# Two attention layers on one core: the last two batches' keys and values made as a pair, four heads at a time

## The chip, the cores and the metric

The kernel runs on one NeuronCore of one Trainium2 chip, in fp32 throughout. The metric is the device time of one execution in microseconds; before the change the median of three runs is 2086.57 us (2086.13 to 2086.70).

## The reference

Two cross-attention layers follow each other. Each has a query projection, keys and values for 77 text tokens and 645 image tokens of the same batch, 20 heads of 32, an output projection and a residual. The second layer adds a semantic term to the image scores and multiplies the image probabilities by a mask. What matters here is this part of each layer (the second layer's weights are not transposed; the text part is a softmax of its own, and its output is added):

```python
q = x @ Wq                     # 8 batches, 100 rows, 640 columns
ip_k = ip @ Wk_ip              # 8 batches, 645 tokens, 1024 -> 640
ip_v = ip @ Wv_ip
scores = einsum('bhqd,bhkd->bhqk', heads(q), heads(ip_k)) * scale
fused = scores + 0.5 * sem     # second layer only
ip_probs = softmax(fused) * mask
ip_out = einsum('bhqk,bhkd->bhqd', ip_probs, heads(ip_v))
out = (text_out + ip_out) @ Wout + bout + x
```

## The kernel before

A **unit** `u` is one layer and batch: units 0 to 7 are the first layer, 8 to 15 the second. A **chunk** `c` is four heads, 128 columns of the 640; there are five. An attention **step** is one unit and chunk, so there are 80 steps, numbered 5u + c. The loop from line 1118 on runs them in order. In a step, TensorE makes the scores of one step in two parts (`scores`, line 850: the first 512 of the 722 tokens, then 210) and, of the step before, the transposes of the probabilities (`transposes`, six of them, line 938) and the product with the values (`values`, line 954). Between the two the softmax runs on VectorE (maxima, factors, rests) and ScalarE (exponentials, scaling by 512 columns), in order on each.

In the gaps of these steps TensorE makes the image keys and values of later units (**production**). They are written to DRAM (`k_d[u]` is 128 x 5 x 645, `v_d[u]` 640 x 640) by GpSimd's DMA queue, and read back chunk by chunk by SyncE's queue (`load_k`, `load_v`, two buffers each).

Units 0 to 13 are produced in **pairs** (`pair_tasks`, line 478), by blocks of 128 tokens (the last 133). Two batches, two halves of the 1024 input columns and two halves of the output columns make a 2 x 2 by 2 x 2 block product, which is done by seven products instead of eight (`seven`, line 159): four sums of the tokens (`token_sums`, line 211: two on VectorE, L212 and L213, two on GpSimd, L214 and L215, in the one buffer `s`), three sums of the weights kept beside the blocks (`weight_sums`, line 126), and after the products two ScalarE copies (L173, L182) and five VectorE adds (L178, L188, L193, L199, L204) that put the results together. One seven-run makes v (products of 4 matmuls by 320 columns, L528), one makes k's first four chunks (8 matmuls by 128 columns, L536), and the fifth k chunk is a plain product (L503).

Units 14 and 15 are produced **plainly**, each alone (`single_tasks`, line 624; `last_tasks`, line 661; matmuls at L608): unit 14's k by 256 columns and v by 320; unit 15's k by 256, and its v chunk by chunk by 128. Chunks 3 and 4 of unit 15 are copied straight into the k and v tiles that attention reads; all else goes through DRAM.

Each product writes a PSUM tile of a pool of two (`ps_pj`); transposes, values, output pieces and the semantic term share another pool of two (`ps_pt`); the scores have one of four banks.

The order on TensorE is written by the kernel (`manual_schedule`). `production` (line 980) gives a plan: stretches of steps, each with a list of tasks and a time for each task; `spread` places the tasks in the stretch so that every step has about the same work. `between` (line 1108) issues, in four gaps of a step, the tasks that are due, and at least one if any falls due within 0.4 of a step. The orders on VectorE, ScalarE, GpSimd and SyncE come from the framework's scheduler. x blocks (two batches, 1.05 MB) come in by SyncE into two buffers.

Output pieces (`out_piece`, line 768) of a pair are made in the second step of the unit that follows it; units 14 and 15 are groups of their own (`GROUPS`), unit 14's pieces come in unit 15's second step, unit 15's are `last_out_begin` and `last_out_end` behind the last step.

Of the kernel before, what the change touches and what calls it, by code (L numbers as in the profile page):

```python
# [38 lines left out]
BIG = [(0, 256), (256, 512), (512, NI)]  # L39
PAIRS = [(2 * i, 2 * i + 1) for i in range(NU // 2 - 1)]  # L40
GROUPS = [list(p) for p in PAIRS] + [[NU - 2], [NU - 1]]

@with_exitstack
def two_layer_xattn(
# [58 lines left out]
    def weight_tile(tag, n, name=None):  # L103
        w = HC + NT if tag in WITH_TEXT else n
        wide[tag] = wpool.tile([P, HK, w], F32, tag=tag, name=name or tag)
        return wide[tag][:, :, :n]
# [313 lines left out]
    group_of = {u: (g, us.index(u)) for g, us in enumerate(GROUPS) for u in us}  # L420
# [15 lines left out]
    def load_k(u, c):  # L436

        l, b = divmod(u, B)
        t = kpool.tile([P, NK], F32, tag="k", name=f"k_{u}_{c}")
        if u < LAST or c < 3:  # L440
            nc.sync.dma_start(t[:, :NI], k_d[u][:, c, :])
        nc.sync.dma_start(t[:, NI:], kt_d[l][c][:, b * NT : (b + 1) * NT])
        ks[u, c] = t
# [21 lines left out]
    def load_res(g):  # L465

        us = GROUPS[g]
        l, b = divmod(us[0], B)
        t = one.tile([P, 2, NC_, S], F32, tag="res", name=f"res_{g}")
        n = len(us)  # L470
        if l == 0:
            nc.sync.dma_start(t[:, :n], x_t[:, b : b + n])
        else:
            nc.sync.dma_start(t[:, :n], x1_d[b // 2][:, b % 2 : b % 2 + n])
        resg[g] = t
# [111 lines left out]
    def big_block(u, m):  # L587

        n0, n1 = BIG[m]
        if m < 2:  # L590
            t = cpool.tile([P, NCC, 2 * NX], F32, tag="x", name=f"x_{u}_{n0}")
        else:
            t = spool.tile([P, NCC, 2 * NX], F32, tag="s", name=f"x_{u}_{n0}")
        nc.sync.dma_start(t[:, :, : n1 - n0], ip_t[u % B].rearrange("k p n -> p k n")[:, :, n0:n1])
        return t

    def plain_product(time, make_dst, n, lhs, rhs, name, then=None):

        parts = 2 if time > 2.5 else 1
        open_ = {}  # L600

        def part(i):
            if i == 0:
                open_["dst"], open_["ps"] = make_dst(), product_ps(name)
            dst, ps = open_["dst"], open_["ps"]
            m = dst.shape[0]
            for k in range(NCC // parts * i, NCC // parts * (i + 1)):
                nc.tensor.matmul(ps[:m, :n], lhsT=lhs(k), rhs=rhs(k), start=(k == 0), stop=(k == NCC - 1))  # L608
            if i == parts - 1:
                nc.scalar.copy(dst, ps[:m, :n])  # L610
                if then:
                    then(dst)

        return [(time / parts, lambda i=i: part(i)) for i in range(parts)]

    def wk_plain(c):
        def w(k):
            if c == 4:
                return W["k", 4][:, k]
            return W["k", f"b{k // HK + 1}{c // 2 + 1}"][:, k % HK, c % 2 * P : (c % 2 + 1) * P]  # L620

        return w

    def single_tasks(u):
        tasks, xs = [], {}

        def begin():
            for m in range(3):
                xs[m] = big_block(u, m)

        def k_one(c, m):
            n0, n1 = BIG[m]
            n = n1 - n0
            return plain_product(
                0.0137 * n, lambda: opool.tile([P, 256], F32, tag="ko", name=f"ko1_{u}_{c}_{m}")[:, :n], n,
                wk_plain(c), lambda k: xs[m][:, k, :n], f"psk1_{u}_{c}_{m}",
                lambda dst: nc.gpsimd.dma_start(k_d[u][:, c, n0:n1], dst),
            )

        def v_one(j, h):  # L640
            at = j % 2 * P
            return plain_product(
                4.3, lambda: opool.tile([P, HC], F32, tag="vo", name=f"vo1_{u}_{j}_{h}"), HC,
                lambda k: xs[j // 2][:, k, at : at + P], lambda k: W["v", f"b{k // HK + 1}{h + 1}"][:, k % HK],
                f"psv1_{u}_{j}_{h}",
                lambda dst: nc.gpsimd.dma_start(v_d[u][j * P : (j + 1) * P, h * HC : (h + 1) * HC], dst),
            )

        tasks.append((0.0, begin))
        for m in range(3):  # L650
            for c in range(NC_):
                tasks += k_one(c, m)
            for j in range(2 * m, min(2 * m + 2, NB)):
                for h in range(2):
                    tasks += v_one(j, h)
        return tasks


    LAST = NU - 1

    def last_tasks():

        u = LAST
        xs, wv = {}, {}

        def begin():
            for m in range(3):
                xs[m] = big_block(u, m)
            for c, (tag, n) in enumerate((("wvt2", HC), ("wvt3", HC), ("wvt4", HC), ("wkt2", 2 * P), ("wkt3", 2 * P))):
                t = weight_tile(tag, n, f"wvl_{c}")  # L670
                t = t[:, :, : 2 * P].rearrange("p a (b n) -> p a b n", b=2)
                src = wvi[1].rearrange("(a b p) n -> p a b n", p=P, b=2)
                for a in range(HK):
                    nc.sync.dma_start(t[:, a], src[:, a, :, c * P : (c + 1) * P])
                wv[c] = t

        def k_one(c, m):
            n0, n1 = BIG[m]
            n = n1 - n0

            def dst():
                if c < 3:
                    return opool.tile([P, 256], F32, tag="ko", name=f"ko1_{u}_{c}_{m}")[:, :n]
                if m == 0:
                    load_k(u, c)
                return ks[u, c][:, n0:n1]

            return plain_product(
                0.0137 * n, dst, n, wk_plain(c), lambda k: xs[m][:, k, :n], f"psk1_{u}_{c}_{m}",
                (lambda t: nc.gpsimd.dma_start(k_d[u][:, c, n0:n1], t)) if c < 3 else None,  # L690
            )

        def v_one(c, j):
            def dst():
                if c < 3:
                    return opool.tile([P, P], F32, tag="vo", name=f"vo1_{u}_{c}_{j}")
                if j == 0:
                    vs[u, c] = vpool.tile([P, NB, P], F32, tag="v", name=f"v_{u}_{c}")
                return vs[u, c][:, j, :]

            at = j % 2 * P
            return plain_product(
                1.8, dst, P, lambda k: xs[j // 2][:, k, at : at + P], lambda k: wv[c][:, k // 2, k % 2],
                f"psv1_{u}_{c}_{j}",
                (lambda t: nc.gpsimd.dma_start(v_d[u][j * P : (j + 1) * P, c * P : (c + 1) * P], t))
                if c < 3 else None,
            )

        return (
            [(0.0, begin)],  # L710
            [[t for m in range(3) for t in k_one(c, m)] for c in range(NC_)],
            [[t for j in range(NB) for t in v_one(c, j)] for c in range(NC_)],
        )

# [53 lines left out]
    def out_piece(g, c):  # L768
        us = GROUPS[g]
# [34 lines left out]
    last_w, last_ps = {}, []  # L804

    def last_out_weights():
        for i, (tag, n) in enumerate((("wv00", HC), ("wv10", HC), ("wv11", HC))):
            weight_tile(tag, n, f"wol_{i}")
# [7 lines left out]
        r = resg[len(GROUPS) - 1][:, 0]  # L816
        nc.gpsimd.tensor_tensor(r, r, bias_sb[:, 1].unsqueeze(2).to_broadcast([P, NC_, S]), ALU.add)

    def last_out(ks_):
        for k in ks_:  # L820
            for c in range(NC_):
                nc.tensor.matmul(
                    last_ps[0][:, c * S : (c + 1) * S], lhsT=last_w[c][:, k, :], rhs=hsg[len(GROUPS) - 1][:, 0, k, :],
                    start=(k == 0 and c == 0), stop=(k == NC_ - 1), skip_group_check=True,
                )

    def last_out_begin():
        last_ps.append(product_ps("pso_last"))
        last_out(range(NC_ - 1))

    def last_out_end():
        last_out([NC_ - 1])
        r = resg[len(GROUPS) - 1][:, 0].rearrange("p c s -> p (c s)")
        nc.vector.tensor_tensor(r, last_ps[0][:, : NC_ * S], r, ALU.add)
        nc.sync.dma_start(out[B - 1], resg[len(GROUPS) - 1][:, 0])
# [118 lines left out]
    def values(u, c):  # L954
        g, at = group_of[u]
        if c == 0 and at == 0:
# [23 lines left out]
    def production():  # L980

        plan = []
        for i in range(1, len(PAIRS)):
            tasks = pair_tasks(PAIRS[i])
            if i == B // 2 - 1:

                at = max(n for n, (t, _) in enumerate(tasks) if t == 2.15) + 1
                tasks = tasks[:at] + [(0.0, lambda: second_weights("v"))] + tasks[at:]
                tasks.append((0.0, lambda: second_weights("k")))
            plan.append((10 * (i - 1) - AHEAD, 10 * i - AHEAD, tasks))  # L990

        def plain_weights():
            for kind, src, n in (("v", wvi[1], HC), ("k", wki[1], 2 * P)):
# [207 lines left out]
```

## Time and profile before

| | |
|---|---|
| median of three runs | 2086.57 us |
| the profiled execution, its own time | 2087.19 us |
| its span | 2085.4 us |
| TensorE busy | 2065.0 us, 99% |
| weight loads (overlapping) | 1630.3 us, 78% |
| VectorE, ScalarE, GpSimd busy | 948.3, 869.3, 333.6 us |
| moved by DMA | 241.96 MB, mean 116 GB/s |
| granted TensorE clock | 1.0 |

A line of a group reads: code line, engine, operation, written tile<-read tiles, shape, number of records; then busy us, mean ns of one; then the engine's idle time before them and what ended it. A matmul in fp32 is two records. "128*128 128x256" is a weight of 128 rows and 128 columns and a moving operand of 128 rows and 256 columns. L numbers are lines of the kernel before. The timeline gives start and length in us of successive records of one kind. The last pair's products end at 1739.5 us, those of unit 14 at 1908 or so, unit 15's at 2068.8.

### The profile page before, as it was taken

To read this page: it belongs to the slowest core of one execution; us is meant where nothing else is said; L and a number is where in the kernel's file an instruction comes from. 1 tells how busy PE (TensorE), PEld (TensorE's weight loads), DVE (VectorE), ACT (ScalarE), POOL (GpSimd) and SP (SyncE) were. 2 spreads that over 40 slices of the span, in tenths; PEclk is the share of its full clock that TensorE was granted. 3 is DMA by queue.
4 is the path that set the end of the run, shared out by engine and by line. 5 is a ranking of instruction groups with operands and counts; after the bars stand their busy time and mean duration, and the time that the engine had idled before them with its cause. 6 is when DMAs were issued, how large, how long until landed. Compare 5 with 4: busy or idle time off the path is not lost.

```text
span 2085.4 us, 40990 instructions
## 1 busy us (share of the span) xinstructions
PE 2065.0 (99%) x16370; PEld 1630.3 (78%) x16370; DVE 948.3 (45%) x2460; ACT 869.3 (42%) x2865; POOL 333.6 (16%) x378
## 2 busy tenths in 40 slices
PE   8999999999999999999999999999999999999998
PEld 8676787777777777787788877887888778777887
DVE  2211221345454554444454554445455454555554
ACT  1001000245434544344444544445444455676765
POOL 3213221111110111111150111111111110101110
PEclk9999999999999999999999999999999999999999
DMA  9345232323334443352544443353244345434320
GB/s 348 111 133 166 87 88 78 114 75 95 104 97 119 122 119 88 96 162 81 154 128 128 124 117 81 109 151 98 80 121 130 96 117 156 145 104 119 112 83 7
DMA packets 272493, 241.96 MB, mean 116 GB/s; under 512 B 42798, under 2 KB 241890, under 8 KB 272302
## 3 DMA queue, kind: packets, MB, share of 16 engines
q1 hardware_dynamic: 253182, 171.97, 30.2%
q0 software_dynamic: 19120, 67.37, 9.6%
q8 instruction: 129, 2.11, 0.4%
q14 instruction: 62, 0.51, 0.1%
HBM read 171.68 MB, written 67.61 MB: 115 GB/s over the span
## 4 chain that ended last, share of the span: by engine, by line
PE 96%; ACT 1%; DVE 1%; issue 0%; DMA 0%; SPq 0%; DVEq 0%; ACTq 0%
PE psv_a L528 8%; PE psv_d L528 8%; PE pspt L945 7%; PE psk_d L536 6%; PE psk_a L536 6%; PE sc L860 6%; PE psk L503 6%; PE pv L967 5%; PE psv_e L528 4%; PE psv L608 4%; PE psk L608 4%; PE psv_b L528 4%; PE psv_c L528 4%; PE psk_b L536 3%; PE psk_e L536 3%; PE psk_c L536 3%
## 5 line engine op out<-in xcount | busy, mean ns | idle before, releaser
L884 ACT ACTIVATE p<-sc,st 100x512 f32<-100x512 f32 (+1 forms) x320 | 166.3, 528 | 225.2 <-DVE st L869 225.1
L952 DVE COPY pt<-pspt 128x400 f32<-128x400 f32 x320 | 176.2, 570 | 170.5 <-PE pspt L945 166.7
L884 ACT ACTIVATE p<-p,st 100x512 f32<-100x512 f32 (+1 forms) x320 | 177.0, 555 | 131.7 <-DVE st L876 131.4
L912 ACT ACTIVATE p<-p,st 100x512 f32<-100x512 f32 x320 | 210.3, 714 | 45.7 <-DVE st L906 45.3
L945 PEld LDWEIGHTS pspt<-ident,p 100*128 100x128 f32 (+1 forms) x1920 | 187.4, 137 | 39.6 <-DVE res L779 6.4
L945 PE MATMUL pspt<-ident,p 100*128 100x100 f32 (+1 forms) x1920 | 211.9, 250 | 6.2 <-DVE res L779 2.8
L528 PE MATMUL psv_a<-wv,x 128*128 128x397 f32 (+1 forms) x560 | 185.2, 473 | 0.0
L950 ACT COPY pt<-pspt 128x400 f32<-128x400 f32 (+1 forms) x160 | 77.9, 487 | 244.2 <-PE pspt L945 243.3
L528 PE MATMUL psv_d<-wv,s 128*128 128x320 f32 (+1 forms) x560 | 174.7, 454 | 0.0
L869 DVE TENSOR_REDUCE st<-sc 100x2 f32<-100x1024 f32 (+1 forms) x120 | 126.2, 1052 | 68.1 <-ACT p L884 37.7
L552 POOL DMA_DIRECT2D v_d<-vo x70 | 39.5, 564 | 721.0 <-DVE gst L520 386.3
L528 PEld LDWEIGHTS psv_a<-wv,x 128*128 128x128 f32 x560 | 103.2, 189 | 63.6 <-issue 9.4
L876 DVE CUSTOM_DVE_ANT_0 p<-sc,sem 100x512 f32<-100x512 f32 (+1 forms) x320 | 139.1, 490 | 28.3 <-PE sc L860 28.3
L528 PEld LDWEIGHTS psv_d<-wv,s 128*128 128x128 f32 x560 | 103.6, 190 | 56.0 <-issue 6.6
L536 PEld LDWEIGHTS psk_a<-x,wk 128*128 128x128 f32 x1120 | 132.3, 191 | 12.7 <-issue 9.4
L536 PE MATMUL psk_d<-s,wk 128*128 128x128 f32 (+1 forms) x1120 | 139.7, 277 | 0.0
L860 PE MATMUL sc<-k,q 32*100 32x210 f32 (+1 forms) x1280 | 138.5, 502 | 1.1 <-ACT p L884 0.6
L536 PE MATMUL psk_a<-x,wk 128*128 128x128 f32 (+1 forms) x1120 | 139.1, 277 | 0.0
L536 PEld LDWEIGHTS psk_d<-s,wk 128*128 128x128 f32 x1120 | 131.2, 191 | 8.2 <-issue 3.3
L564 POOL DMA_DIRECT2D k_d<-ko x70 | 58.1, 829 | 463.7 <-DVE ko L199 438.0
L503 PE MATMUL psk<-x,wk 128*128 128x256 f32 (+1 forms) x560 | 131.6, 383 | 0.0
L503 PEld LDWEIGHTS psk<-x,wk 128*128 128x128 f32 x560 | 102.1, 189 | 23.2 <-issue 7.9
(180 smaller groups left out, 3299.3 us busy)
## 6 DMA issues: line engine op xcount, KB each, us to landing
x<-ip_t SPq DMA_DIRECT2D x56, 512.0 KB
k<-k_d SPq DMA_DIRECT2D x78, 322.5 KB
v<-v_d SPq DMA_DIRECT2D x78, 320.0 KB
v_d<-vo POOLq DMA_DIRECT2D x70, 320.0 KB, 2.6
k_d<-ko POOLq DMA_DIRECT2D x56, 320.0 KB, 7.0
o<-wo SPq DMA_DIRECT2D x40, 320.0 KB
x<-ip_t SPq DMA_DIRECT2D x16, 532.0 KB
q<-wq SPq DMA_DIRECT2D x20, 320.0 KB
```

Source lines behind the costliest of these rows:

```text
L503: nc.tensor.matmul(ps[:, : 2 * n], lhsT=W["k", 4][:, k, :], rhs=xs[j][:, :, k, :n], start=(k == 0), stop=(k == NCC - 1),)
L528: nc.tensor.matmul(ps[:, :m], lhsT=sums[which][:, k, :P], rhs=w[:, k, :], start=(k == 0 and not go_on), stop=(k == HK - 1), skip_group_che ...
L536: nc.tensor.matmul(ps[:, r * n : (r + 1) * n], lhsT=W["k", WHICH[which]][:, k, r * P : (r + 1) * P], rhs=sums[which][:, k, :], start=(r == ...
L608: nc.tensor.matmul(ps[:m, :n], lhsT=lhs(k), rhs=rhs(k), start=(k == 0), stop=(k == NCC - 1))
L860: nc.tensor.matmul(sc[:S, i, : k1 - k0], lhsT=qs_[u][rows, c, :], rhs=ks[u, c][rows, k0:k1], start=True, stop=True)
L869: nc.vector.tensor_reduce(st[:, part, heads[0] : heads[-1] + 1], sc[:S, heads[0] : heads[-1] + 1, :n], AX.X, ALU.max, negate=True,)
L876: nc.vector.tensor_tensor_reduce(out=p[:, i, k0 : k0 + n], in0=sc[:S, i, :n], in1=sems[u][:, k0 : k0 + n], scale=-1.0, scalar=3.0e38, op0= ...
L884: nc.scalar.activation(dst, dst if l else sc[:S, i, :n], AF.Exp, bias=st[:, part, i : i + 1], scale=-1.0 if l else 1.0, accum_out=st[:, 3 ...
L912: nc.scalar.activation(p[:, i, :KA], p[:, i, :KA], AF.Copy, scale=mul[:, 0, i : i + 1])
L945: nc.tensor.transpose(ps[:rows, i * S : (i + 1) * S], pr[u, c][:, i, j * P : j * P + rows], ident[:S, :S])
L952: nc.vector.tensor_copy(dst, src)
L967: nc.tensor.matmul(ps[32 * i : 32 * i + 32, :S], lhsT=lhs, rhs=pt[:rows, j, i * S : (i + 1) * S], start=(j == 0), stop=(j == 5),)
```

## The change

Units 14 and 15 become an eighth pair. Their k and v chunks 0 to 3 are made by seven products, but **by two chunks**: `two_chunks(r, ...)` makes chunks r and r + 2 (one from each half of the first 512 output columns) of both k and v, for r = 0 over all five blocks and then for r = 1. Each of its seven products is 4 matmuls of 128 columns for v and 4 for k (128 or 133 columns) into one PSUM tile. So the x blocks are read twice and the token sums made twice. The **fifth chunk** is plain (`fifth_chunk`): k for all five blocks, with v for the first two (x is read a third time), then v for blocks 2, 3 and 4 (a fourth time). Everything goes through DRAM.

The attention of the last ten steps is in another order (`ORDER`): chunks 0 and 2 of unit 14, 0 and 2 of unit 15, then 1 and 3 of each, then the fifth of each. The v weights are loaded anew for the 512-column split (`last_weights`, in the k products of the last block of units 12 and 13) and summed on GpSimd. The semantic term of unit 15 is made in step 70 instead of in steps 73 and 74. The output pieces of both units are 50 matmuls of 100 columns in and behind the last step (`last_out`).

```diff
-BIG = [(0, 256), (256, 512), (512, NI)]
-PAIRS = [(2 * i, 2 * i + 1) for i in range(NU // 2 - 1)]
-GROUPS = [list(p) for p in PAIRS] + [[NU - 2], [NU - 1]]
+PAIRS = [(2 * i, 2 * i + 1) for i in range(NU // 2)]
+
+ORDER = [(u, c) for u in range(NU - 2) for c in range(NC_)]
+ORDER += [(u, c) for cs in ((0, 2), (1, 3), (4,)) for u in PAIRS[-1] for c in cs]
...
+    LAST = PAIRS[-1]
+
+    def last_weights():
+        load_quarters("v", wvi[1], 2 * P)
+        for h, tag in enumerate(("wv00", "wv10")):
+            nc.sync.dma_start(
+                wide[tag][:, :, 2 * P : 3 * P],
+                wvi[1].rearrange("(k p) n -> p k n", p=P)[:, HK * h : HK * (h + 1), 4 * P :],
+            )
+        weight_sums("v", 2 * P, (nc.gpsimd, nc.gpsimd))
+
+    def blocks_of(js, tasks_of):
+
+        xs, tasks = {}, []
+        for i, j in enumerate(js):
+
+            def begin(i=i, j=j):
+                if i == 0:
+                    xs[j] = load_x(LAST, *BLOCKS[j])
+                if i + 1 < len(js):
+                    xs[js[i + 1]] = load_x(LAST, *BLOCKS[js[i + 1]])
+
+            tasks += [(0.0, begin)] + tasks_of(j, xs)
+        return tasks
+
+    def two_chunks(r, j, xs):
+        n0, n1 = BLOCKS[j]
+        n = n1 - n0
+        sums, o, made = {}, {}, {}
+
+        def begin():
+            x = xs[j][:, :, :, :n]
+            t = spool.tile([P, 4, HK, NX], F32, tag="s", name=f"sl_{r}_{j}")
+            a11, a12, a21, a22 = (x[:, i, HK * h : HK * (h + 1)] for i in range(2) for h in range(2))
+            sums.update(token_sums(a11, a12, a21, a22, *(t[:, i, :, :n] for i in range(4))))
+            o[0] = opool.tile([P, 2, 2, P + NX], F32, tag="ko", name=f"vko_{r}_{j}")
+
+        def product(ps, which, go_on):
+            for k in range(HK):
+                nc.tensor.matmul(
+                    ps[:, :P], lhsT=sums[which][:, k, :P], rhs=W["v", WHICH[which]][:, k, r * P : (r + 1) * P],
+                    start=(k == 0 and not go_on), stop=(k == HK - 1), skip_group_check=True,
+                )
+            for k in range(HK):
+                nc.tensor.matmul(
+                    ps[:, P : P + n], lhsT=W["k", WHICH[which]][:, k, r * P : (r + 1) * P], rhs=sums[which][:, k, :],
+                    start=False, stop=(k == HK - 1), skip_group_check=True,
+                )
+
+        def step(i):
             if i == 0:
...
+                made[0] = seven(
+                    f"psvk_{r}_{j}", product, tuple(o[0][:, h, m, : P + n] for h in range(2) for m in range(2))
+                )
+            made[0][i]()
+            if i < 6:
+                return
+            for h, u in enumerate(LAST):
+                nc.gpsimd.dma_start(
+                    k_d[u][:, :4, n0:n1].rearrange("p (m r) n -> p r m n", r=2)[:, r], o[0][:, h, :, P : P + n]
+                )
+                nc.gpsimd.dma_start(
+                    v_d[u][j * P : (j + 1) * P, : 4 * P].rearrange("p (m r n) -> p r m n", m=2, r=2)[:, r],
+                    o[0][:, h, :, :P],
+                )
...
+        return [(0.0, begin)] + [(1.8, lambda i=i: step(i)) for i in range(7)]
+
+    def fifth_chunk(kinds, j, xs):
...
+            def half(h, kind=kind, n=n, open_=open_):
...
+                if kind == "k":
+                    for k in range(HK * h, HK * (h + 1)):
+                        nc.tensor.matmul(
+                            ps[:, : 2 * n], lhsT=W["k", 4][:, k, :], rhs=xs[j][:, :, k, :n],
+                            start=(k == 0), stop=(k == NCC - 1),
+                        )
+                else:
+                    for k in range(NCC):
+                        nc.tensor.matmul(
+                            ps[:, h * P : (h + 1) * P], lhsT=xs[j][:, h, k, :P],
+                            rhs=wide[("wv00", "wv10")[k // HK]][:, k % HK, 2 * P : 3 * P],
+                            start=(h == 0 and k == 0), stop=(k == NCC - 1), skip_group_check=True,
+                        )
...
     def production():
 
         plan = []
-        for i in range(1, len(PAIRS)):
+        for i in range(1, len(PAIRS) - 1):
             tasks = pair_tasks(PAIRS[i])
...
+            elif i == len(PAIRS) - 2:
+                tasks = tasks[:at] + [(0.0, last_weights)] + tasks[at:]
             plan.append((10 * (i - 1) - AHEAD, 10 * i - AHEAD, tasks))
...
+        n = 5 * LAST[0]
+        every = list(range(NB))
+        by_chunks = [blocks_of(every, lambda j, xs, r=r: two_chunks(r, j, xs)) for r in range(2)]
+        fifth = [
+            blocks_of(every, lambda j, xs: fifth_chunk("kv" if j < 2 else "k", j, xs)),
+            blocks_of(every[2:], lambda j, xs: fifth_chunk("v", j, xs)),
         ]
+        plan.append((n - 10 - AHEAD, n + 2.9, by_chunks[0] + by_chunks[1]))
+        plan.append((n + 2.9, n + 6.9, fifth[0]))
+        plan.append((n + 6.9, n + 8.6, fifth[1]))
         return [task for a, b, tasks in plan for task in spread(a, b, tasks)]
...
+        if n == len(ORDER) - 1:
+            for i in range(2):
+                for ks_ in ((0, 1), (2, 3)):
+                    at[2 * i + ks_[0] // 2].append((2.3, lambda i=i, ks_=ks_: last_out(i, ks_)))
...
+        for n, (u, c) in enumerate(ORDER):
+            at = small_work(n)
+            loads(n)
+            scores(u, c, 0)
+            if n == len(ORDER) - 1:
+                load_v(*last)
+                load_v(u, c)
...
-        last_out_begin()
+        last_out(0, [NC_ - 1])
         for j in range(6):
             transposes(*last, j)
         values(*last)
-        last_out_end()
+        last_out(1, [NC_ - 1])
```

## The prediction

> **What bounds the kernel now.** I read the busy times first, then who TensorE waited for, then TensorE's own order of work by time. The first line of the page, and the three longest waits in the whole run:
>
> ```profile
> PE 2065.0 (99%) x16370; PEld 1630.3 (78%) x16370; DVE 948.3 (45%) x2460; ACT 869.3 (42%) x2865; POOL 333.6 (16%) x378
> ...
> PE psq L252 <- DMA wq<-wq: 5.6, 1, 5.6
> PE pspt L945 <- DVE res L779: 2.8, 15, 0.3
> PE pv L967 <- DVE pt L952: 1.7, 5, 0.6
> ```
>
> TensorE (PE) is the bound everywhere: outside the start and the last 11 us it hardly waits. So the change is worth the matmul time it removes, less every wait that it creates. The products it replaces are one line, L608, and lie after 1740 us (groups of the window 1740 to 2081; each fp32 matmul is two records):
>
> ```profile
> L608 PE MATMUL psk<-x,wk 128*128 128x256 f32 x320 | 77.8, 386 | 0.0
> L608 PE MATMUL psv<-wvl,x 128*128 128x128 f32 x400 | 49.5, 278 | 0.0
> L608 PE MATMUL psv<-wv,x 128*128 128x320 f32 x160 | 47.6, 440 | 0.0
> L608 PE MATMUL psk<-x,wk 128*128 128x133 f32 x160 | 20.0, 278 | 0.0
> ```
>
> That is 160, 200, 80 and 80 matmuls, 194.9 us busy. These records overlap at their ends, so I take prices from starts in the timeline (start, duration, what):
>
> ```profile
> 1683.73 1.95 PE L536 MATMUL psk_b<-s,wkt 128*128 128x128 f32 x16
> 1685.51 1.95 PE L536 MATMUL psk_a<-x,wk 128*128 128x128 f32 x16
> ...
> 1705.46 2.32 PE L528 MATMUL psv_b<-wvt,s 128*128 128x320 f32 x8
> 1707.61 2.32 PE L528 MATMUL psv_a<-wv,x 128*128 128x320 f32 x8
> ...
> 1756.69 1.89 PE L608 MATMUL psk<-x,wk 128*128 128x256 f32 x8
> 1758.42 0.85 PE L945 MATMUL pspt<-ident,p 100*128 100x100 f32 x8
> ...
> 2069.94 4.71 PE L822 MATMUL pso_last<-hs,wol 128*128 128x100 f32 x40
> 2074.49 0.85 PE L945 MATMUL pspt<-ident,p 100*128 100x100 f32 x8
> ```
>
> A 128-wide matmul costs 1.78/8 = 0.223 us, a 320-wide 2.15/4 = 0.5375, a 256-wide 1.73/4 = 0.4325. In the same view a 133-wide one is 1.83/8 = 0.229 and a 266-wide one 3.70/8 = 0.4625.
>
> **The products.** Before: 160 x 0.4325 + 80 x 0.5375 + 200 x 0.223 + 80 x 0.229 = 69.2 + 43.0 + 44.6 + 18.3 = 175.1 us. After: two chunk pairs x 5 blocks x 7 products x 8 matmuls = 560, of them 504 at 128 and 56 at 133 columns (112.4 + 12.8); the fifth chunk's k is 32 at 256 and 8 at 266 (13.8 + 3.7), its v 80 at 128 (17.8). Sum 160.5 us. **Saved: 14.6 us.** With the groups' busy per matmul instead (0.248 for 128 columns, 0.25, 0.466, 0.489) it is 194.9 - 177.8 = 17.1; 14.6 to 17.1 are the ends, and I take the starts, since they are real time.
>
> [...] The change has 640 narrow matmuls (128 or 133) for 280 now. [...] 16 records of 128 columns and 128 rows start within 1.78 us, 111 ns each, load included. [...] the 100-wide last row above still takes 4.55/40 = 114 ns a record. [...] I use 0.223.
>
> **What else goes.** Batch 14's own five output pieces (L774, 100 wide) move to the end as 25 matmuls at the same 111 to 114 ns a record, so no gain there; but the transposes between them now queue for the PSUM buffers and take 1.14 instead of 0.85 us, four times: **-1.1 us**. The second attention stage itself (scores, transposes, values, 80 steps) and the sem work are unchanged in number.
>
> **The chunk stage** (70 products over 14 attention steps). A step's own TensorE work is 4.9 us: the step below lasts 12.28 with 7.34 of products in it.
>
> ```profile
> 2025.73:2038.01 12.28, 12.28 (x133) 9.93 (x129) 8.07 (x30) 8.06 (x31) 1.11 (x2) 1.00 0.22 56
> ...
> 1656.00:1658.00 2.00, 2.00 (x56) 1.10 (x48) 1.97 (x3) 0.00 (x0) 1.97 (x2) 1.00 1.08 299
> 1658.00:1660.00 2.00, 2.00 (x13) 1.75 (x10) 2.00 (x7) 0.61 (x1) 1.36 (x2) 1.00 1.08 346
> ```
>
> (Stretches: length, busy of PE, PEld, DVE, ACT, POOL, clock, DMA share, GB/s.) With 125 us of products, a chunk-stage step is 125/14.1 + 4.9 = 13.8 us, like the 13.5 to 14 us steps of batch 14's making, which run without a gap. New there are the sums of the next block at each of ten boundaries: `s` has one buffer, so the sum on VectorE (1.38 us, L212) and the difference (0.72, L213) start only when the last product is done, and the second product needs them. Cover: the first product, 1.8, and an attention piece of about 1 us; need: 0.4 for the last add, 2.1 for the two, and the queue of VectorE. GpSimd has four stores (about 0.55 each) and then 1.3 (L214) before the fourth product. Today two k halves (3.6 us) and a 2.15 us product stand there. From 0 to 0.6 us each; with 0.2: **+2.0 us** (0 to 6). VectorE's 50 new adds (0.43 each) and ScalarE's 20 copies (0.38) add 1.5 and 0.5 us a step to about 9 each of 13.8, so they stay off the path. The new v weights (4 x 512 KB, 2 x 256 KB) are asked for when the last pair's v products end at 1721, and 18 us of k products and attention cover them and the first two of GpSimd's four sums (2.36 each, by L131's row at 1024 columns); at the layer change the same arrangement cost no wait. Zero, or 3 us if that cover is gone.
>
> **The fifth chunk** is where I expect the loss. Its 14 + 6 half tasks lie in 5.7 steps, so a step has 3.5 x 1.8 + 4.9 = 11.2 us. x is read again (eight loads of 1.05 MB). The buffers are two, so block j+1 is asked for when block j-1 is done; where blocks hold only two tasks, that leaves 3.6 + 2.4 = 6.0 us. Five loads are so (blocks 3 and 4 of the first pass, 2, 3, 4 of the second). The nearest row: a pair of x loads issued at 1653.6 beside a v load and two stores, 2.03 MB, kept the DMA engines full until 1662 at 282 to 346 GB/s. Here it is 1.05 MB, half of a step's k and v (0.33) and a store (0.13): 1.5 MB at 0.29 MB a us = 5.2, plus 1.5 for issue and landing = 6.7. Late by 0.7 each: **+3.5 us**. [...] Bounds: 0 and 10.
>
> In those steps ScalarE has about 9.4 of 11.2 us. From the second scores to the scaled rows is 7.8 us today (2031.9 to 2039.75). A step with four tasks gives 9.0 us for it, one with three 7.2 plus; half of the steps have three. **+1.5 us** (0 to 6). Batch 15's k and v chunks 3 and 4, made straight into their tiles before, now go through DRAM: copy 0.37, store 0.54 and 2.1 to land, load about 2.5, some 6 us against more than one step (11 us): hidden. The output weights asked for four steps before the end have 45 us.
>
> **The tail** is the same but for the last row of batch 14's output, which waits for its values (0.4, as pso_last does now), and an add of 0.68 ahead of the copies: **+0.5 us**.
>
> **Sum:** -14.6 - 1.1 + 2.0 + 3.5 + 1.5 + 0.5 = -8.2 us. The profiled execution took 2087.19 (span 2085.4 and 1.8 around it): 2079.0. The median of the runs is 0.6 lower, so **2078.4**, 0.4% faster.
>
> **Rivals.** *Everything hides* (chunk sums, loads, softmax): -15.2, or -17.7 at the groups' price: 2071.4 to 2068.9. For it: TensorE waited under 6 us in all of 1740 to 2070. *ScalarE becomes the bound in the last steps*: 12.3 instead of 11.2 us for 5.7 steps, +6.3 for my 1.5: 2083. For it: 84% load in a chain; against: single steps of 10.9 and 11.0 us show a wait of only 0.33. *The x loads eat it*: 1.6 late each, +8: 2083. *Slower*: the same five loads queue on SyncE behind k or v loads that wait for attention (SP stood up to 19 us at L441, 9.6 at L447). Without the loads' term the sum is -11.7, so it decides against the change from (11.7 + 4.2)/5 = 3.2 us late each; at 4 us it gives 2095. Against it: today's x loads stand in the same queue and were missed once in 76. That the products aren't removed is excluded by the counts in the code.
>
> **How the numbers follow.** Mine 0.55 (its own range 2074 to 2082), everything hides 0.20, ScalarE 0.09, loads 0.10, slower 0.06. Faster by over 0.2% (below 2082.4; that is about what these runs can tell) is 0.75, within 0.19, slower 0.06. The range 2070 to 2086 reaches over the first three rivals, and leaves out the lowest end of the first and the slower case.
>
> **What would show it.** PE records 16370 + 2 x (680 - 520) = 16690; products after 1740 us some 14.6 us shorter by starts; waits of PE for DVE s or POOL s at chunk boundaries (2 us), for DMA x in the last 80 us (3.5), for ACT p at the transposes (1.5). I am wrong if 128-wide products with v and k in one PSUM tile run slower than 1.8 us, if waits for x exceed 8 us or are absent, or if a k or v load is late.

## The result, and the profile after

The changed kernel takes 2084.48 us (median of 20 runs, 2080.15 to 2088.13), the kernel before beside it 2087.45 (20 runs, 2086.13 to 2089.47). The ratio is **0.9985**, 95% interval 0.9978 to 0.9991: 3.0 us faster where 8.2 were forecast, less than the 0.2% that was set as the bound for a difference. It lies in the wide range (2070 to 2086) and outside the likeliest case's own (2074 to 2082). Its runs spread over 8 us, those of before over 3.3.

The profiled execution is the slowest of the 20: 2088.13 us, span 2086.4, mean granted clock 0.996 (before: 2087.19, 2085.4, 1.000). The busy line of the page:

```profile
PE 2058.5 (99%) x16690; PEld 1641.6 (79%) x16690; DVE 988.3 (47%) x2526; ACT 862.8 (41%) x2830; POOL 379.8 (18%) x409
```

The 16690 records are those forecast, 320 more, and TensorE is busy 6.5 us less, not 15.7. Here are the products in TensorE's timeline (start, duration, what):

```profile
1753.98 1.08 PE L627 MATMUL psvk_d<-wv,sl 128*128 128x128 f32 x8
1754.90 1.06 PE L632 MATMUL psvk_d<-sl,wk 128*128 128x128 f32 x8
1755.79 0.85 PE L922 MATMUL pspt<-ident,p 100*128 100x100 f32 x8
```

The halves of a product start at 1753.98 and 1754.90, the next work at 1755.79: 1.81 us for the two, as priced (1.78). So the removed time is not eaten by dearer products. Whom TensorE waited for after 1740 us (engine, tile, line, awaited engine and tile: us in all, times, longest):

```profile
PE pso L752 <- DMA o<-wo: 3.0, 2, 2.4
PE pspt L922 <- DVE pt L929: 2.5, 2, 1.9
PE psvk_b L627 <- DVE sl L214: 1.0, 2, 0.8
...
PE pso_last L804 <- DVE hs L948: 0.8, 2, 0.4
...
PE psk L669 <- DMA x<-ip_t: 0.5, 2, 0.3
```

The forecast waits are small: 1.0 for the token sums, 0.5 for x, 0.8 in the tail. The two on top had no term: the output pieces in step 61 (those of units 10 and 11) wait for their weights, and a transpose of step 78 waits 1.9 us for its softmax. Soon after that wait the same instructions take twice as long (TensorE's timeline):

```profile
2048.54 1.12 PE L837 MATMUL sc<-k,q 32*100 32x512 f32 x8
2049.59 0.48 PE L922 MATMUL pspt<-ident,p 100*128 100x100 f32 x3
2050.24 0.65 PE L922 MATMUL pspt<-ident,p 100*128 100x100 f32 x5 [0.18 <-ACT p L889]
2052.80 1.04 PE L922 MATMUL pspt<-ident,p 100*128 100x100 f32 x8 [1.90 <-DVE pt L929]
...
2056.67 1.90 PE L944 MATMUL pv<-pt,v 128*32 128x100 f32 x40 [0.58 <-ACT pt L927]
2058.34 0.56 PE L944 MATMUL pv<-pt,vt 82*32 82x100 f32 x8
2058.83 2.04 PE L837 MATMUL sc<-k,q 32*100 32x512 f32 x8
```

Step 78 runs from 2048.54 to 2058.83 and holds no product at all: 10.29 us for some 4.9 of its own work. The scores that open it take 1.12 us, those that open the next step 2.04. The table of stretches shows why (length, busy of PE, PEld, DVE, ACT, POOL, granted clock, DMA share, GB/s):

```profile
2050.00:2052.00 2.00, 0.71 (x6) 0.46 (x5) 2.00 (x7) 1.74 (x6) 0.00 (x0) 1.00 0.18 50
2052.00:2054.00 2.00, 1.20 (x12) 0.98 (x16) 1.34 (x5) 1.88 (x5) 0.00 (x0) 1.00 0.49 146
2054.00:2056.00 2.00, 2.00 (x16) 1.29 (x12) 1.83 (x11) 0.89 (x4) 0.00 (x0) 0.52 0.00 0
2056.00:2058.00 2.00, 1.42 (x33) 1.33 (x36) 0.84 (x5) 1.87 (x10) 0.00 (x0) 0.50 0.03 8
2058.00:2060.00 2.00, 2.00 (x32) 0.96 (x24) 1.17 (x7) 1.02 (x7) 0.00 (x0) 0.50 0.06 14
2060.00:2062.00 2.00, 2.00 (x17) 1.20 (x11) 1.67 (x4) 2.00 (x4) 0.00 (x0) 0.78 0.51 150
```

In the first two stretches TensorE has work for 1.91 of 4 us; then the granted clock is halved for some 7 us. TensorE counts as busy for most of that time, so neither the busy share nor the table of waits shows this loss. It happens three times: from 1790 to 1796 (behind the output pieces), from 1948 to 1956 (behind step 70) and here. Before, no stretch of 2 us between 1740 and 2070 us is below 1.00.

The output pieces' timeline, before and then after:

```profile
1779.38 3.55 PE L774 MATMUL pso<-hs,o 128*128 128x200 f32 x20
...
1784.45 1.93 PE L774 MATMUL pso<-hs,o 128*128 128x200 f32 x10 [0.43 <-DMA o<-wo]
...
1787.93 0.81 PE L608 MATMUL psv<-wv,x 128*128 128x320 f32 x2
```

```profile
1783.25 3.55 PE L752 MATMUL pso<-hs,o 128*128 128x200 f32 x20
...
1790.30 2.76 PE L752 MATMUL pso<-hs,o 128*128 128x200 f32 x10 [2.42 <-DMA o<-wo]
1792.86 1.65 PE L922 MATMUL pspt<-ident,p 100*128 100x100 f32 x8
...
1795.07 1.16 PE L627 MATMUL psvk_a<-wv,x 128*128 128x128 f32 x8
```

The third piece's weights come 2 us later than before, and the stretch takes 11.82 instead of 8.55 us. While they were awaited the DMA engines were full, 346 GB/s from 1784 to 1786 and 297 from 1788 to 1790. SyncE issued a pair of x loads at 1779.3, 6 us ahead of these weights at 1785.1, and GpSimd stored four pieces of the new products, 128 KB each, two of them at 1784.8 and 1785.5. In the 16 us around them the queues moved 3.33 MB, at the same place in the kernel before 2.01, without any x load and with one such store of 160 KB. Which of the two holds the weights up was not varied.

**Where it went.** Both kernels can be cut at the first product of the last two units (1740.35 before, 1742.41 after). Ahead of it the changed kernel is 2.06 us behind; that is one wait, told of at the end. From it to the end of the span, before takes 345.05 us and after 343.99: 1.06 us shorter in this execution, where 8.2 were forecast.

### The profile page after: what moved, and what is told of

Same layout as the page of the kernel before. It is cut to its first block, busy times and chain, and to the rows that moved or that the text cites. A ratio compares the mean times of both kernels' runs of the same rounds, so it can differ in the third digit from the quotient of the medians.

```text
span 2086.4 us, 41767 instructions
## 1 busy us (share of the span) xinstructions
PE 2058.5 (99%) x16690; PEld 1641.6 (79%) x16690; DVE 988.3 (47%) x2526; ACT 862.8 (41%) x2830; POOL 379.8 (18%) x409
## 5 line engine op out<-in xcount | busy, mean ns | idle before, releaser
L552 POOL DMA_DIRECT2D v_d<-vo x70 | 39.5, 564 | 723.6 <-DVE gst L520 386.4
```

## The experiments

The question is whether the missing gain lies in the steps that were left without a product (a hole and the halved clock behind it), or in ScalarE's load over all the last steps, which would cost the same wherever products stand. Each kernel is compared with the kernel before, run beside it.

**Step 78 filled with products.** The two stretches of the fifth chunk are drawn out, so that the last v tasks fall later:

```diff
-        plan.append((n + 2.9, n + 6.9, fifth[0]))
-        plan.append((n + 6.9, n + 8.6, fifth[1]))
+        plan.append((n + 2.9, n + 7.3, fifth[0]))
+        plan.append((n + 7.3, n + 8.95, fifth[1]))
```

> The changed kernel with one edit: the fifth chunk's two stretches end later, so that two of the last v tasks fall into step 78, which had none. Holes theory (a step without product tasks leaves TensorE waiting on transposes and their copies, and the clock then runs at one half for some 6 us): step 78 has 2 x 1.8 us more work and yet takes about 9.5 us instead of 10.3, step 77 gives up as much work, no stretch at clock 0.50 around 2050 to 2060; 3 to 5 us less in all, about 2080.5. Softmax theory (the last steps wait for ScalarE, 9.4 of 11.2 us a step): moving tasks between steps changes nothing beyond 1 us, about 2084.5.

Measured: 2078.52 us (5 runs, 2076.5 to 2079.26), ratio 0.9954 (0.9942 to 0.9967): 8.3 us faster than before. Nothing but the place of tasks differs from the changed kernel. TensorE's timeline of step 78:

```profile
2037.39 1.12 PE L837 MATMUL sc<-k,q 32*100 32x512 f32 x8
2038.44 2.05 PE L675 MATMUL psv<-wv,x 128*128 128x128 f32 x16
...
2045.96 1.07 PE L944 MATMUL pv<-pt,v 128*32 128x100 f32 x40 [0.89 <-ACT pt L927]
...
2048.06 1.12 PE L837 MATMUL sc<-k,q 32*100 32x512 f32 x8 [0.86 <-ACT p L875]
```

The step now holds two v tasks (about 3.7 us) and lasts 10.67 us (9.5 were expected), hardly more than the 10.29 without any, and the scores after it take 1.12 us. Steps 74 to 78 take 55.6 us together instead of 59.2: 3.7 us, about the two tasks that found room in step 78. From step 79 to the end of the span it is 26.6 instead of 27.6. So the chain of softmax sets the length of such a step, and products in it cost nearly nothing.

**Step 78 filled with useless work.** To separate the clock from the placing, the changed kernel gets four groups of four 128-wide matmuls in that step, 3.6 us of work; nobody reads what they compute:

```diff
+        if n == len(ORDER) - 2:
+            for i in range(4):
+                at[i].append((0.0, lambda i=i: filler(i)))
...
+    def filler(i):
+        ps = product_ps(f"fill_{i}")
+        for k in range(4):
+            nc.tensor.matmul(
+                ps[:, :P], lhsT=W["k", 4][:, k, :], rhs=W["k", 4][:, k + 4, :], start=(k == 0), stop=(k == 3),
+            )
```

> The changed kernel with useless work added: in each of the four gaps of step 78 four 128-wide matmuls whose result nobody reads, 3.6 us in all. If the loss there is idle time alone (2.7 us of waits are recorded), filling it costs 3.6 - 2.7 = 0.9 us: 2085.4. If the clock is what is lost, the filler keeps it at 1.0, the 3 to 4 us at half speed are saved as well: 2 to 3 us faster than the changed kernel, about 2082, with more work. If the softmax chain bounds the step, the filler hides in it: 2084.5.

Measured: 2080.92 us (6 runs, 2078.53 to 2083.55), ratio 0.9968 (0.9956 to 0.9980): 5.9 us faster than before, 2.9 better than the changed kernel with 3.6 us more to do. The intervals of the two touch (0.9978 to 0.9980), so the size of this gain is loose; a loss of 3.6 us, which added work would be if TensorE had no idle time there, is ruled out. The clock is 1.00 in every stretch from 1740 to 2070 us, the longest wait left in step 78 is 0.45 us, and the step lasts 9.67 us, from 2043.48 to 2053.15, shorter than the 10.29 without the filler:

```profile
2047.74 1.04 PE L922 MATMUL pspt<-ident,p 100*128 100x100 f32 x8 [0.45 <-DVE pt L929]
...
2053.15 1.12 PE L837 MATMUL sc<-k,q 32*100 32x512 f32 x8
```

**Step 70 and the semantic term.** The logits one gap later, the rest in step 71:

```diff
-            at[1].append((0.9, lambda: sem_logits(z)))
-            at[2].append((0.2, lambda: sem_transpose(z)))
-            for i in range(2):
-                at[3].append((0.6, lambda i=i: sem_scores(z, i)))
+            at[2].append((0.9, lambda: sem_logits(z)))
+        if n == NC_ * LAST[0] + 1:
+            at[0].append((0.2, lambda: sem_transpose(z)))
...
+                if u == LAST[0]:
+                    at[2].append((0.6, lambda: sem_scores(z, 0)))
+                    at[3].append((0.6, lambda: sem_scores(z, 1)))
```

> The changed kernel with one edit: unit 15's semantic term is spread over steps 70 and 71, so that the third gap of step 70 has a product task. Holes theory: the half clock around 1948 to 1955 goes, steps 70 and 71 together 3 to 5 us shorter, about 2080.5. Softmax theory: the same as the changed kernel, 2084.5 within 1. Should both holes be needed to hold the clock back, this and the run before each give less than 2 us.

Measured: 2080.56 us (5 runs, 2079.48 to 2081.6), ratio 0.9966 (0.9954 to 0.9979): 6.2 us faster than before, 3.2 better than the changed kernel, whose interval (0.9978 to 0.9991) this one overlaps. `spread` counts the small tasks as work that fills a step, so with the whole semantic term in step 70 that step's last two gaps got no product. Its timeline in the changed kernel's profile:

```profile
1946.56 0.99 PE L922 MATMUL pspt<-ident,p 100*128 100x100 f32 x8
1948.17 2.41 PE L734 MATMUL psm<-g,tpt 77*100 77x323 f32 x4 [0.62 <-ACT pt L927]
1950.51 1.90 PE L944 MATMUL pv<-pt,v 128*32 128x100 f32 x40
```

The semantic scores take 2.41 us there and 1.33 in executions in which the clock stays. In this experiment's profile only the stretch behind step 78 (2044 to 2052 us) is below 1.00. Steps 70 and 71 take 35.5 us in it, against 39.5 in the changed kernel's profile. But where the changed kernel keeps its clock at step 70, as in its second profile below, they take 37.0, so in such an execution the edit is worth 1.5 us and the rest of the 3.2 isn't shown to come from it.

**The output pieces in steps 61 and 71 apart** (in unit 12 those of units 10 and 11, in unit 14 those of units 12 and 13). There are two weight buffers and two pieces stood in one gap, so the third piece's weights could be asked for only once the first was done, shortly before they were needed:

```diff
-                    at[(0, 0, 1, 2, 3)[i]].append((1.7, lambda c=c: out_piece(g, c)))
+                    at[((0, 1, 2, 3, 3) if u > 10 else (0, 0, 1, 2, 3))[i]].append((1.7, lambda c=c: out_piece(g, c)))
```

> The changed kernel with one edit: the five output pieces of units 12 and 14 lie in gaps 0, 1, 2, 3, 3 instead of 0, 0, 1, 2, 3, so that the third one's weights have longer to land. Load theory (the x load of the new blocks holds the DMA engines from 1780 to 1790, and the output weights queue behind it): the wait of 2.4 us for them and the half clock behind it go, 3 us less, about 2081.5. If it was chance of one execution: no change, 2084.5.

Measured: 2080.23 us (5 runs, 2077.55 to 2080.49), ratio 0.9960 (0.9948 to 0.9973): 6.6 us faster than before, 3.6 better than the changed kernel. The wait for `o` is gone from its table. Step 61 takes 22.35 us; without the edit it takes 26.0 and 26.1 in the two profiles in which its clock falls (waits of 2.42 and 2.3 us for `o`), and 23.5 to 24.0 in the three in which it stays (waits of 1.3 to 1.8). The clock is below 1.00 only behind step 78, from 2042 to 2050. Step 70 is as in the changed kernel, with the same waits of 0.43 and 0.62 us, and kept its clock in this execution.

**The changed kernel again**, in another session, to see which of the three places are there each time.

> The changed kernel as it is, once more, beside the next two on the same chip, for a profile of an ordinary execution. About 2084.5 (its 20 runs lie between 2080.2 and 2088.1). Holes theory: the half clock in step 78 is in every execution, that of step 70 and behind the late output weights only in some, and that is what spreads the times; the profile then has 5 to 9 us less of full clock than its length. Softmax theory: clock near 1.0 in some execution of the same length.

Measured: 2084.43 us (16 runs, 2082.63 to 2085.68), ratio 0.9982 (0.9974 to 0.9989). Halved clock behind the output pieces (1786 to 1792) and behind step 78 (2046 to 2058), none behind step 70. Its timeline there, with the same wait:

```profile
1945.75 1.33 PE L734 MATMUL psm<-g,tpt 77*100 77x323 f32 x4 [0.62 <-ACT pt L927]
1947.07 1.06 PE L944 MATMUL pv<-pt,v 128*32 128x100 f32 x40
```

So step 70 is a place where the clock falls in some executions and not in others.

**All three edits together**, with the semantic scores in gaps 1 and 2 of step 71.

> The changed kernel with the three edits together: the fifth chunk later, unit 15's semantic term over two steps, the output pieces apart. Holes theory: the gains add, about 6.0 + 3.9 + 4.3 = 14 us less than the changed kernel, less what two holes share: 2071 to 2074, which is the kernel before less the 14.6 us of products that were taken away. If each edit only happened to save the same variable loss, the three together give no more than the best alone, 2078.5.

Measured: **2073.77 us** (5 runs, 2073.21 to 2076.38), ratio **0.9935** (0.9923 to 0.9948): 14.1 us faster than before and 11.1 better than the changed kernel. Taken singly the edits gave 5.3, 3.2 and 3.6, 12.1 in all: they add up within what five runs can tell. It beats both kernels, and its instructions are those of the changed one in another order. Two of its five runs (2075.86 and 2076.38) have a mean clock of 0.999 and 0.998 where the others have 1.000, so the clock seems to fall in some executions still. The profiled execution's busy line:

```profile
PE 2050.2 (99%) x16690; PEld 1636.9 (79%) x16690; DVE 984.1 (47%) x2526; ACT 861.7 (42%) x2830; POOL 379.6 (18%) x409
```

and TensorE's longest waits after 1740 us:

```profile
PE pv L944 <- DVE pt L929: 1.2, 4, 0.4
PE psvk_b L627 <- DVE sl L214: 1.0, 2, 0.8
PE pv L944 <- ACT pt L927: 0.9, 1, 0.9
```

As many records as in the changed kernel, 8.3 us less busy, near the 8.5 us of full-clock time that the changed kernel's profile lost: the slow clock had stood under "busy". Against before it is 14.8 us less busy. The longest wait after 1740 us is 0.9.

**The hole alone, in the kernel before.** Nothing of the change is in it; unit 15's last tasks are drawn together so that its step 78 is left without a product:

```diff
-            (n + 1.65, n + 2.65, k[3]),
-            (n + 2.65, n + 3.4, k[4]),
-            (n + 3.4, n + 4.3, v[3]),
-            (n + 4.3, n + 5, v[4]),
+            (n + 1.3, n + 2.2, k[3]),
+            (n + 2.2, n + 2.9, k[4]),
+            (n + 4.4, n + 4.7, v[3]),
+            (n + 4.7, n + 5, v[4]),
```

> The kernel before with its tasks moved and none removed: unit 15's last k chunks earlier, its last v chunks into the last step, so that step 78 has no product task, as in the changed kernel. Holes theory: the same loss without seven products by chunks: clock 0.50 for about 6 us behind step 78, 5 to 6.5 us slower than the kernel before, about 2092. If the loss belongs to the new products or to the DRAM round trips of the fifth chunk: no slower than 2088.

Measured: 2094.17 us (6 runs, 2093.53 to 2097.95), ratio 1.0034 (1.0022 to 1.0046): **6.3 us slower** than before, with the same work. Its timeline in and behind the hole:

```profile
2042.57 1.12 PE L860 MATMUL sc<-k,q 32*100 32x512 f32 x8
...
2046.83 1.04 PE L945 MATMUL pspt<-ident,p 100*128 100x100 f32 x8 [0.97 <-DVE pt L952]
...
2050.61 1.90 PE L967 MATMUL pv<-pt,v 128*32 128x100 f32 x40 [0.58 <-ACT pt L950]
...
2052.77 2.04 PE L860 MATMUL sc<-k,q 32*100 32x512 f32 x8
```

The same picture as in the changed kernel, here without its products, loads or sums. So the hole is enough. (One new wait lies outside it: 0.5 us of a k product for a copy by ScalarE.)

**One table for the last stage.** Time from the first product of the last two units to the end of the span, in each profile (one execution each), and the full-clock time lost in it: the sum over 2-us stretches from 1740 to 2070 us of (1 - clock) x 2.

| kernel | stage, us | lost by the clock, us |
|---|---|---|
| before | 345.05 | 0 |
| hole in before | 351.7 | 3.4 |
| changed | 343.99 | 8.5 |
| changed again | 342.3 | 6.8 |
| step 78 filled by products | 334.4 | 0 |
| filler in step 78 | 337.5 | 0 |
| semantic term in two steps | 337.0 | 3.4 |
| output pieces apart | 336.1 | 3.4 |
| three edits | 331.7 | 0 |

The second column doesn't hold the idle time that precedes each fall. It is also more than what a fall costs, since part of the slow stretch lies in steps in which TensorE would otherwise have waited for the softmax (steps 70 and 71: 2.5 us longer for 3.4 in the column). And single executions differ in which places fall: the profile of the first edit happened to keep its clock at the other two places, so its stage (9.6 us under the changed kernel's) flatters it against the 5.3 of the medians. By steps, the three edits' profile is shorter than the changed kernel's first (second) one by 3.6 (3.7) us in step 61, 4.0 (1.6) in steps 70 and 71, 3.7 (3.8) in steps 74 to 78, and 1.0 (1.4) from step 79 on.

## Why the prediction was wrong

**The price of the products: right.** Forecast 14.6 us, by starts rather than by busy time. With the holes closed the medians are 14.1 apart and the stage is 13.4 shorter, with some 2 us of small new waits in it. The 16 records of a product pass in 1.81 us, their weight loads included, where 1.78 was taken.

**Transposes between the last output pieces, -1.1:** no run tells it apart from the products; together the two were forecast at 15.7.

**The token sums, +2.0:** 1.0 waited, twice, within the bounds of 0 to 6.

**The x loads, +3.5: mis-sized**, in the work that covers them and not in the loads. They waited 0.5 in all. The two loads that TensorE waited for, as SyncE issued them and as TensorE came to use them (two timelines):

```profile
2008.38 1.01 SPq L149 DMA_DIRECT2D x<-ip_t  x2
2014.96 0.99 SPq L149 DMA_DIRECT2D x<-ip_t  x2
...
2015.86 1.97 PE L669 MATMUL psk<-x,wk 128*128 128x256 f32 x8 [0.23 <-DMA x<-ip_t]
2021.97 2.03 PE L669 MATMUL psk<-x,wk 128*128 128x266 f32 x8 [0.30 <-DMA x<-ip_t]
```

From issue to use they took 7.5 and 7.0 us, a little more than the 6.7 that were reckoned from the busier place (1.5 of them, for issue and landing, the author's estimate). But TensorE had other work for 7.25 and 6.7 of them instead of 6.0, and the other three loads of the five came in time.

**The tail, +0.5:** 0.8 waited for `hs`.

**The step that failed** is the one that stood ahead of the x loads: "Its 14 + 6 half tasks lie in 5.7 steps, so a step has 3.5 x 1.8 + 4.9 = 11.2 us." That is a mean over steps, and the plan doesn't give it. A stretch that ends at n + 8.6, with tasks drawn up to 0.4 of a step ahead, puts four of the last six v tasks in step 77 and none in step 78. The ScalarE term (+1.5) spoke of steps with three or four tasks, and in those last steps only 0.2 us was waited for `p`; a step with none was never considered, and it alone waited 1.9 and 0.6 us at the end of its softmax chain, with a slow clock behind it. Filling it gained 5.3 us, making it in the kernel before cost 6.3. The same holds for step 70, where "the sem work are unchanged in number" was taken to mean unchanged in cost, though the change brought it together in one step, and for the output pieces in step 61, whose weights now share the DMA engines with x loads and new stores: the forecast counted a delay of loads for x alone, not for `o`.

**What was missing altogether** is the clock. Every price was a full-clock price. In the changed kernel's two profiles the halved clock takes 8.5 and 6.8 us of full-clock time; that is the upper end of what it cost, and two places show the cost itself. Steps 70 and 71, with the same instructions, took 39.5 us in the profile in which the clock fell there and 37.0 in the one in which it stayed: 2.5 us for 3.4 of full-clock time. Step 78 and what follows it took 37.9 and 39.1 us in these profiles and 36.2 with the filler: 1.6 and 2.9 us less, with 3.6 us more to do, for 3.4 and 5.1 of full-clock time. So the clock is a large part of the 11.1 us between the changed kernel and the three edits. The rest is waits and the room in step 78, and no run splits the sum exactly.

**The rivals.** "Everything hides" (2071.4 to 2068.9) is nearly what the three edits reach: the products allow it, the placing didn't. "ScalarE becomes the bound in the last steps" gave 2083, near the measured 2084.5, but for a wrong reason: its load is the same in the kernel with the fifth chunk drawn out, which is 5.3 us faster. What is true of it is that the softmax chain sets the length of a step with few or no products (10.3 to 10.7 us). "The x loads eat it" and "slower" fall with the 0.5 us of waits for x.

## What to carry to other kernels

When work is taken out of a stage or moved within it, list which step each remaining piece lands in, gap by gap; the mean over steps hides the one that gets none. A step whose other chain is longer than TensorE's work is free room: pieces put there cost almost nothing (3.7 us of products made step 78 longer by 0.4), and a step left empty costs its room and then, here, another 1.6 to 2.9 us by the slower clock behind it. Look at the granted clock in short stretches wherever waits lie close together, since time lost that way is booked as busy (8.3 us of it here); waits of 0.43 and 0.62 us, within 3.3 us of each other, stood ahead of a fall in one execution of step 70, and the same two brought none in another.

## What the runs showed of the hardware

**The clock falls without a long idle stretch.** The longest single waits ahead of a fall were 2.42 us (output pieces), 1.90 (step 78), 0.97 (hole in before) and 0.62 (step 70); one such place took 1.7 to 5.1 us of full-clock time. In the changed kernel's profile the clock goes from 1.00 to 0.50 at 1791.25, 1948.26 and 2054.07 us and stays there for 3.41, 6.83 and 6.83 us; values between stand only in stretches that hold both. The falls are 157.01 and 105.81 us apart, 46 and 31 times 3.413 (a 46th of the first distance). In the 3.41 us just ahead of them TensorE was busy for 0.29, 0.69 and 0.44 of the time, less than in any other such piece of 1740 to 2070 us, counted in steps of 3.413 from the first fall (the next has 0.77). The length of the waits alone doesn't decide it. In step 70 TensorE waits 0.43 and then 0.62 us in both profiles of the changed kernel, and the clock falls in the first and stays in the second. Counted in the same way from the second profile's fall at 1787.4, the two waits lie in different pieces, and the one with the 0.62 has 0.82 busy. In the profile of the first edit TensorE waits 1.37 us for `o` before 1787.16, and 0.89 and 0.86 us before 2045.96 and 2048.06, and the clock stays at 1.00 up to 2070. So what sets off a fall is not shown: no run varied what TensorE does in such a piece, and that the pieces decide is the author's estimate. The changed kernel's 8 us of spread goes with it: its three fastest runs (2080.2 to 2081.7 us) have a mean clock of 0.998 or 0.999, and its five slowest (2085.75 to 2088.13) have 0.996.

**A VectorE instruction of 0.7, 2.0 or 4.3 us.** Ahead of the last stage the changed kernel's profile has one wait in a stretch whose instructions are those of before. TensorE, VectorE and GpSimd there (three timelines):

```profile
1067.62 2.42 PE L528 MATMUL psv_a<-wv,x 128*128 128x320 f32 x8 [1.96 <-ACT vo L174]
...
1060.20 4.26 DVE L897 TENSOR_TENSOR p<-p,st 100x532 f32<-100x532 f32 x1
...
1060.16 1.43 POOL L216 TENSOR_TENSOR s<-x,s 128x512 f32<-128x512 f32 x1
1061.40 2.48 POOL L132 TENSOR_TENSOR wkt<-wk,wk 128x1024 f32<-128x1024 f32 x1
1063.96 2.70 POOL L133 TENSOR_TENSOR wkt<-wkt,wk 128x1024 f32<-128x1024 f32 x1
```

The product of 100 x 532 takes about 0.7 us elsewhere, 1.8 to 2.0 at this place in seven of the nine profiles and 4.26 or 4.28 in two. In the changed kernel's profile it starts just after GpSimd's L216 and ends 0.58 us after the next one, L132, which follows L216 at once. In the profile of before it starts just after the same sum (L215 there) and ends 0.58 us after that one; GpSimd's next sum starts 1.16 us later there, since its weights have yet to land. In both, then, it ends 0.58 us after a sum of GpSimd's; no run moved those sums away, so the cause isn't shown.
